# An attention kernel's opening: a load call moved, one root by GpSimd, six roots in two batches

## Chip, cores and metric

The kernel runs on one core of a Trainium2 chip. The metric is the device time of one execution in microseconds (us); lower is better. The engines are TensorE (PE; its weight loads are shown as PEld), VectorE (DVE), ScalarE (ACT) and GpSimd (POOL); SyncE (SP) issues most of the DMA transfers.

## The reference, cut

The input `x` has the shape (2, 256, 128, 128): batch, times, bands, channels, all float32.

```python
xt = _ln(x, ln_t_w, ln_t_b).transpose(0, 2, 1, 3)
x = x + _mha(xt, t_wi, t_bi, t_wo, t_bo, 4, causal_mask).transpose(0, 2, 1, 3)   # over times
xf = _ln(x, ln_f_w, ln_f_b)
x = x + _mha(xf, f_wi, f_bi, f_wo, f_bo, 4, band_mask)                           # over bands
xn = _ln(x, ln_n_w, ln_n_b)
h = gelu(xn @ w1.T + b1)                                                         # 128 -> 512
x = x + (h @ w2.T + b2)
```

`_ln` subtracts the mean over the 128 channels and multiplies by the reciprocal root of the variance plus 1e-5. That reciprocal root is "the root" in what follows.

## The kernel before, in words

The work is cut into groups of 512 tokens (128 partitions, four tiles of 128 channels). There are 128 groups of attention over times (`OverTime`), then, in runs, 128 of attention over bands and 128 of the feed-forward part. This document concerns the first dozen groups. Groups are counted from 0 in the code; "fifth group" is `groups[4]`.

**Loads.** `groups()` walks over the bands with `f0` in steps of `GA = 8`. Eight bands are one *quad*: one tile `x`, shared by four groups. Each of the four calls of `load` fetches 32 of its 128 partitions, so the statistics of any group of a quad need all four transfers. Quad 0 (groups 0 to 3) lies in a constant tile, quad 1 (groups 4 to 7) has `f0 = 8`, quad 2 (groups 8 to 11) has `f0 = 16`. `start` calls the loads of quads 0 and 1, then `load_w1T`, then those of quad 2. All these transfers are issued by SP, which works through its list in order.

**Normalising.** For each group, `statistics` (VectorE: four `bn_stats`, four `bn_aggr`) writes mean and variance to `mv`. The root is made in one of two ways. `root` uses GpSimd (add, then power -0.5) and gives `rstd` at once. `root_by_scalar` uses ScalarE (Ln, then Exp with scale -0.5), and `refine` adds a Newton step of three VectorE instructions. The result of ScalarE can be put into a PSUM bank: `root_in_spare` uses the last columns of the bank called `b2`, `root_in_bank` its first columns. A `Four` joins the statistics of several groups in one tile `mvs`, so that one root and one `refine` serve them all; before the change it is used from group 12 on, for four groups each. The early groups are turned (transposed) by TensorE and copied to `xnT` by VectorE; from group 4 on (`TURNED`) a group goes through VectorE's 32x32 transpose and DRAM (`turned`), and is fetched back as `xnT`.

**Steps.** After `start`, `run` emits one step per `n`. A step interleaves the second half of group n's scores with the first half of group n+1's (`time_scores`), the exponentials (`first_weights`, `second_weights`), masks and adds by GpSimd, the products of the weights with the values of group n-1 (`weigh`), its division (`invert` on ScalarE, `divide` on VectorE), and the query, key and value products of group n+2. Eight PSUM banks are passed round by name; after each step `hand_banks_on` gives the names to other banks, so that the next step's scores go into banks that earlier results have left. All engines' instructions are pinned: each engine works through its list in the order in which the program emits it. Line 900 of the profile is the helper that emits them, so tiles and not lines tell the groups apart.

In step 0 the places concerned are, in this order: the late `second_weights`, the fifth root in spare columns, the TensorE turn of group 2 and its copy, the three small products `fold_output` and `fold_hidden` (weights `t_woT`, `f_woT`, `w1T`), the VectorE results `b` and `orow` of these, and `refine` of the fifth group. `stay_warm(4, ...)` in `start` emits 16 matmuls of one column each, whose result is not read.

Of the kernel before, what the change touches and what calls it, by code (L numbers as in the profile page):

```python
# [10 lines left out]
F32 = mybir.dt.float32  # L11
# [8 lines left out]
P = 128  # L20
# [5 lines left out]
NT = 4  # L26
# [6 lines left out]
BANK = 512  # L33
# [336 lines left out]
class Group:  # L370
# [28 lines left out]
    def means(self):  # L399
        if self.four is None:  # L400
            return self.path.small.tile([P, NT, 2], F32, name="mv", bufs=16)
        if self is self.four.groups[0]:
            self.four.mv = self.path.small.tile([P, NT * NT, 2], F32, name="mvs", bufs=3)
        return self.four.part(self.four.mv, self)

    def root(self):
# [21 lines left out]
    def refine(self):  # L428

        path, vector, y, n = self.path, self.path.vector, self.root0, self.mv.shape[1]  # L430
        t = path.small.tile([P, n], F32, name=f"vy{n}")
        vector.scalar_tensor_tensor(t, self.mv[:, :, 1], EPS, y, ALU.add, ALU.mult)
        vector.scalar_tensor_tensor(t, t, -0.5, y, ALU.mult, ALU.mult)
        self.rstd = path.small.tile([P, n], F32, name="rstd" if n == NT else "rstds", bufs=16 if n == NT else 3)
        vector.scalar_tensor_tensor(self.rstd, t, 1.5, y, ALU.add, ALU.mult)

    def normalize(self):
# [200 lines left out]
def rows_of(h):  # L638
    return slice(h * D, (h + 1) * D)


def product(path, out, weights, x, start=True, stop=True, turn=0):


    for c in range(P // D):
        path.tensor.matmul(out[rows_of(c)], weights[:, rows_of((c + turn) % NT)], x, start=start, stop=stop)
# [258 lines left out]
class BoundedPath:  # L905
# [71 lines left out]
    def groups(self, x, out):  # L977
        nc, k = self.nc, self.k
        B, T, FB, C = x.shape
        NC_T = T // P  # L980
        for b in range(B):
            for f0 in range(0, FB, GA):
                held = {}


                def load(g, f0=f0, b=b, held=held):
                    if b == f0 == 0:
                        held["x"] = k.x0
                        return
                    if g == 0:  # L990
                        self.input_quad(held)
                    f = f0 + g // NC_T * NT
                    self.sync.dma_start(held["x"][rows_of(g)], self.of_times(x[b], g, slice(f, f + NT)))

                def store(g, f0=f0, b=b, held=held):
                    for i in range(NT if g % 2 else 0):
                        f = f0 + i // NC_T * NT + g
                        self.sync.dma_start(
                            self.of_times(k.x1[b], i, slice(f - 1, f + 1)), held["res"][rows_of(i), :, g - 1 : g + 1]
                        )  # L1000

                def part(name, g, i=None, a=0, held=held):
                    if name == "res" and name not in held:
                        self.quad(held, "res", 2)
                    if i is not None:
                        return self.longer(held[name], i * NT + g, a)
                    return held[name][:, :, g]

                for g in range(NT):
                    yield OverTime(self, partial(part, "x", g), partial(part, "res", g), partial(load, g), partial(store, g))  # L1010
        for b in range(B):
            for r0 in range(0, T, RUN):
                run = []
                for t0 in range(r0, r0 + RUN, GB):
                    held = {}


                    def load(g, t0=t0, b=b, held=held):
                        if g == 0:
                            self.input_quad(held)  # L1020
                            self.quad(held, "x2", 2 * RUN // GB)
                        self.sync.dma_start(
                            held["x"][rows_of(g)].rearrange("q g t c -> q (g t) c"),
                            self.of_bands(k.x1[b], t0 + NT * g, NT),
                        )

                    def store(g, t0=t0, b=b, held=held):
                        last = b == B - 1 and t0 == T - GB
                        n = 1 if last and g > 1 else 2
                        for i in range(NT if (g + 1) % n == 0 else 0):  # L1030
                            queue = self.scalar if last and g == NT - 1 and i % 2 else self.sync
                            queue.dma_start(
                                self.of_bands(out[b], t0 + NT * i + g + 1 - n, n),
                                held["res"][rows_of(i), g + 1 - n : g + 1].rearrange("q g t c -> q (g t) c"),
                            )

                    def part(name, g, i=None, a=0, held=held):
                        if name == "res" and name not in held:
                            self.quad(held, "res", 2)
                        if i is not None:  # L1040
                            return self.longer(held[name], g * NT + i, a)
                        return held[name][:, g]

                    run += [(g, part, load, store) for g in range(NT)]
                for g, part, load, _ in run:
                    yield OverBands(self, partial(part, "x", g), partial(part, "x2", g), partial(load, g))
                for g, part, _, store in run:
                    yield FeedForward(self, partial(part, "x2", g), partial(part, "res", g), None, partial(store, g))

    def warm(self, banks):  # L1050


        for i in banks:
# [2 lines left out]
            self.tensor.matmul(  # L1056
                bank, self.k.ones, self.k.ident.unsqueeze(1).to_broadcast([P, n, P]), start=True, stop=True
            )

    def stay_warm(self, n, column):  # L1060
        for i in range(n):
            product(self, column, self.k.ident, self.k.ones[:, 0:1])

    def fold(self, a, engine):

# [129 lines left out]
    def start(self, groups):  # L1195

        first, second, third, fourth, fifth = groups[:5]
        b = self.banks
        for group in groups[: 2 * NT]:
            group.load()  # L1200
        self.k.load_w1T()
        for group in groups[2 * NT : 3 * NT]:
            group.load()
        self.warm((0, 1, 5, 2))
        first.statistics()
        self.fold(0, self.vector)
# [26 lines left out]
        time_scores(None, first)  # L1233
        second.turn_by_tensor(b["b0"], self.vector)
        self.fold_products(1, self.ps[7])
        self.stay_warm(4, self.ps[7][:, BANK - 1 :])
        self.fold_bias(1)
        Attention.place = dict(qp=b["b3"], kp=b["b1"], vp0=b["b0"], vp1=b["b2"])
        first.first_weights(first.early)
# [10 lines left out]
        second.values()  # L1250
        second.take_values()
        fifth.statistics()
        self.hand_banks_on()

    def hand_banks_on(self):
# [5 lines left out]
    def run(self, x, out):  # L1261
        groups = list(self.groups(x, out))

        def do(n, *names):
            if 0 <= n < len(groups):
                for name in names:
                    getattr(groups[n], name)()

        def at(n, kind):
            return 0 <= n < len(groups) and isinstance(groups[n], kind)  # L1270
# [10 lines left out]
        run0 = [i for i in range(len(groups)) if at(i, OverBands)][: RUN // NT]  # L1281
        times = range(3 * NT, run0[-1] + 1)
        fours = {i + NT - 1: Four(self, groups[i : i + NT]) for i in times[::NT]}
        A, k = RUN // NT, self.k
        early = [i for i in range(3, len(groups)) if at(i, FeedForward) and at(i - 3, OverBands)]

# [11 lines left out]
        for n in range(len(groups) + 2):  # L1298
# [8 lines left out]
            do(n, "first_half", "first_function", "first_mask")  # L1307
            if n == 0:
                do(3, "normalize_flat")
            if 0 < n < 3 * NT - 5:  # L1310
                do(n + 5, "statistics")
            if n + 2 * NT in times:
                do(n + 2 * NT, "statistics")
            if old is not None or new is not None:
                time_scores(old, new)
                b = self.banks
# [2 lines left out]
                Attention.place = {}  # L1319
            if old is not None:  # L1320
                old.second_weights(old.late)
                if n == 0:
                    do(4, "root_in_spare")
                if n + 2 < TURNED:
                    groups[n + 2].turn_by_tensor(b["b0"], self.vector)
                if n == 0:
                    self.fold_output(self.ps[b["b3"]])
                    self.fold_hidden(b["b3"])
                    self.add_rows()
                    do(4, "refine")  # L1330
                if n == run0[0] - 1:
                    self.square_queries()
                do(n - 2, "output")
# [7 lines left out]
            if new is not None:  # L1341
                new.first_weights(new.early[1:])
            if n == 1:
                do(5, "root_in_spare", "refine")
            if 0 < n < 3 * NT - 5:
                do(n + 5, "root_in_bank")
            if n + 2 * NT in fours:
                fours[n + 2 * NT].root_in_bank()
            if n == run0[0] - 1:
# [15 lines left out]
            if old is not None:  # L1365
                do(n - 2, "finish")
            if n == 0:
                do(5, "statistics")
            elif n + 5 < 3 * NT:
                do(n + 5, "refine")  # L1370
            if n + 2 * NT in fours:
                fours[n + 2 * NT].refine()
            if not bands[2] and not turn:
# [112 lines left out]
```

## Time and profile before

| | |
|---|---|
| median of 3 runs | 2644.02 us (2640.17 to 2646.56) |
| the profiled execution | 2645.2 us |
| its span, first to last instruction | 2643.3 us |
| granted TensorE clock, mean | 0.998 |
| TensorE busy | 2625.4 us, 99% of the span |
| VectorE / ScalarE / GpSimd busy | 2143.1 / 1839.8 / 1955.0 us |
| DMA | 344.99 MB, mean 131 GB/s |
| loads of `x` by SP (256 KB each) | 124, median 4.4 us to landing |

The page gives totals over the span; the timeline and the windows show stretches of it in us from the first instruction. A bracket such as `[2.07 <-ACT p L900]` tells how long an engine stood idle before the row and which event ended that. "issue" means that the profile shows nothing that the engine waited for.

### The profile page before, as it was taken

To read this page: it belongs to the slowest core of one execution; us is meant where nothing else is said; L and a number is where in the kernel's file an instruction comes from. 1 tells how busy PE (TensorE), PEld (TensorE's weight loads), DVE (VectorE), ACT (ScalarE), POOL (GpSimd) and SP (SyncE) were. 2 spreads that over 40 slices of the span, in tenths; PEclk is the share of its full clock that TensorE was granted. 3 is DMA by queue.
4 is the path that set the end of the run, shared out by engine and by line. 5 is a ranking of instruction groups with operands and counts; after the bars stand their busy time and mean duration, and the time that the engine had idled before them with its cause. 6 is when DMAs were issued, how large, how long until landed. Compare 5 with 4: busy or idle time off the path is not lost.

```text
span 2643.3 us, 156538 instructions
## 1 busy us (share of the span) xinstructions
PE 2625.4 (99%) x68720; PEld 1872.0 (71%) x68720; DVE 2143.1 (81%) x6422; ACT 1839.8 (70%) x3553; POOL 1955.0 (74%) x2309
## 2 busy tenths in 40 slices
PE   8999999999999999999999999999999999999998
PEld 5667667666666666777667777777776777777776
DVE  7888888888888887977878779788797797887974
ACT  6898998988998974664755746647557466475573
POOL 6999999999999986666567666665776666657762
PEclk9999999999999999999999999999999999999999
DMA  5655555656656544444454444444444445444443
GB/s 144 156 148 153 156 145 151 160 147 151 155 149 155 128 126 114 121 126 123 119 125 125 122 121 121 127 124 119 121 122 130 118 115 132 125 116 126 117 107 83
DMA packets 469846, 344.99 MB, mean 131 GB/s; under 512 B 43168, under 2 KB 404512, under 8 KB 469152
## 3 DMA queue, kind: packets, MB, share of 16 engines
q1 hardware_dynamic: 468432, 334.41, 49.9%
q8 instruction: 541, 8.86, 1.5%
q14 instruction: 153, 1.25, 0.2%
q10 hardware_dynamic: 720, 0.46, 0.1%
HBM read 167.98 MB, written 166.72 MB: 127 GB/s over the span
## 4 chain that ended last, share of the span: by engine, by line
PE 99%; DVE 0%; issue 0%; DMA 0%; ACT 0%; ACTq 0%; DVEq 0%
PE bank L900 99%; ACT hT L900 0%; DMA x<-in_x 0%; DMA xnT<-turned 0%; DVE stats L900 0%; DVE res L900 0%; DVE u L900 0%; DVE bank L900 0%; ACT p L900 0%; DVE gs L900 0%; DVE mv L900 0%; DVE z L900 0%; DVE oT L900 0%; DVE xnT L900 0%; DVE vy L900 0%
## 5 line engine op out<-in xcount | busy, mean ns | idle before, releaser
L900 ACT ACTIVATE hT<-bank,b 128x512 f32<-128x512 f32 x512 | 347.7, 688 | 516.2 <-PE bank L900 475.4
L900 POOL TENSOR_SCALAR_AFFINE_SELECT pf<-pf 128x512 f32<-128x512 f32 x768 | 476.6, 634 | 184.5 <-ACT pf L900 158.3
L900 PEld LDWEIGHTS bank<-w2T_sb,hT 128*32 128x32 f32 x16384 | 475.5, 110 | 49.5 <-issue 28.9
L900 PE MATMUL bank<-xnT,wf 128*32 128x512 f32 x4096 | 494.4, 594 | 2.2 <-ACT p L900 2.1
L900 PE MATMUL bank<-xnT,w1f 128*32 128x512 f32 x4096 | 494.5, 592 | 0.0
L900 PE MATMUL bank<-w2T_sb,hT 128*32 128x128 f32 x16384 | 490.3, 273 | 1.2 <-issue 0.6
L900 ACT ACTIVATE p<-bank 128x512 f32<-128x512 f32 (+1 forms) x1024 | 430.8, 494 | 71.7 <-PE bank L900 69.2
L900 DVE TENSOR_SCALAR xh<-x,mv,rstd 128x160 f32<-128x160 f32 (+1 forms) x1040 | 405.3, 432 | 59.8 <-POOL rstd L900 49.3
L900 POOL TENSOR_SCALAR_AFFINE_SELECT p<-p 128x1024 f32<-128x1024 f32 (+2 forms) x384 | 363.4, 946 | 67.8 <-ACT p L900 59.5
L900 PEld LDWEIGHTS bank<-wf,xnT 128*32 128x32 f32 x8192 | 244.1, 110 | 145.0 <-issue 100.6
L900 POOL TENSOR_TENSOR p<-p,p 128x512 f32<-128x512 f32 x256 | 324.1, 1287 | 10.7
L900 DVE BATCH_NORM_STATS2 stats<-x 128x6 f32<-128x128 f32 x1536 | 329.1, 277 | 3.3 <-DMA x<-in_x 3.3
L900 POOL TENSOR_SCALAR rstd<-mv 128x4 f32<-128x4 f32 x250 | 57.1, 228 | 362.9 <-DVE mv L900 361.3
L900 PEld LDWEIGHTS bank<-xnT,w1f 128*32 128x32 f32 x4096 | 206.2, 110 | 153.4 <-issue 94.9
L900 PE MATMUL bank<-qT,kT 32*64 32x80 f32 (+4 forms) x16384 | 305.8, 272 | 2.8 <-issue 2.4
L900 PEld LDWEIGHTS bank<-qT,kT 32*64 32x64 f32 x16384 | 261.9, 131 | 55.4 <-ACT kT L900 50.4
L900 DVE TENSOR_TENSOR res<-bank,res 128x512 f32<-128x512 f32 (+1 forms) x259 | 170.4, 658 | 154.1 <-PE bank L900 149.5
L900 ACT ACTIVATE pf<-bank 128x512 f32<-128x512 f32 x512 | 266.2, 601 | 36.2 <-PE bank L900 31.3
L900 PE MATMUL bank<-wn,oT 128*32 128x128 f32 x8192 | 286.9, 274 | 1.0 <-issue 0.9
L900 DVE STREAM_TRANSPOSE z<-xh 128x512 f32<-128x512 f32 x380 | 270.4, 712 | 13.7
L900 PE MATMUL bank<-wf,xnT 128*32 128x128 f32 x8192 | 277.3, 273 | 0.2 <-DVE rstd L900 0.2
L900 POOL TENSOR_TENSOR rstd<-rstd,mhalf 128x4 f32<-128x4 f32 x250 | 259.5, 1038 | 20.8
(102 smaller groups left out, 3825.5 us busy)
## 6 DMA issues: line engine op xcount, KB each, us to landing
turned<-z SPq DMA_DIRECT2D x1520, 64.0 KB, 2.7
xnT<-turned SPq DMA_DIRECT2D x380, 256.0 KB, 3.1
x<-res SPq DMA_DIRECT2D x256, 128.0 KB, 2.4
x<-x SPq DMA_DIRECT2D x128, 256.0 KB, 4.0
out<-res SPq DMA_DIRECT2D x252, 128.0 KB, 2.4
x<-in_x SPq DMA_DIRECT2D x124, 256.0 KB, 4.4
x<-in_x SPq DMA_DIRECT2D x4, 128.0 KB, 2.8
x<-in_x SPq DMA_DIRECT2D x6, 64.0 KB, 2.5
```

What stands on the lines that cost most here:

```text
L900: return self.tc.keep_in_program_order(emit(*args, **kwargs))
```

## The change

- `stay_warm` and its call are removed.
- The loads of quad 2 are no longer called in `start`, but in step 0, after the TensorE turn of group 2. In `load`, a VectorE memset of one column of the fresh `x` tile is emitted when `f0 == 2 * NT`, that is when `f0 == 8`.
- The fifth group's root is made by GpSimd in `start`; its ScalarE root and its `refine` in step 0 are removed.
- Groups 5 to 7 and groups 8 to 10 form two batches of three, with one root and one `refine` each (steps 1 and 3); group 11 has its own (step 5). The statistics of groups 5 to 11 are emitted at other places: group 5 in step 0 after the turn, 6 and 7 at the end of step 0, 8 in step 1, 9 to 11 in steps 2 to 4.
- The tiles `mvs` and `rstds` are always taken at full size and cut to the number of groups.

```diff
-            self.four.mv = self.path.small.tile([P, NT * NT, 2], F32, name="mvs", bufs=3)
+            mvs = self.path.small.tile([P, NT * NT, 2], F32, name="mvs", bufs=3)
+            self.four.mv = mvs[:, 0 : NT * len(self.four.groups)]
...
                     if g == 0:
                         self.input_quad(held)
+                        if b == 0 and f0 == 2 * NT:
+                            self.vector.memset(held["x"][:, 0, 0, 0:1], 0.0)
...
         self.k.load_w1T()
-        for group in groups[2 * NT : 3 * NT]:
-            group.load()
...
         self.fold_products(1, self.ps[7])
-        self.stay_warm(4, self.ps[7][:, BANK - 1 :])
...
         fifth.statistics()
+        fifth.root()
...
+        threes = [Four(self, groups[i : i + 3]) for i in (5, 8)]
...
-            if 0 < n < 3 * NT - 5:
-                do(n + 5, "statistics")
+            if 1 < n < 5:
+                do(n + 7, "statistics")
...
-                if n == 0:
-                    do(4, "root_in_spare")
                 if n + 2 < TURNED:
                     groups[n + 2].turn_by_tensor(b["b0"], self.vector)
                 if n == 0:
+                    for group in groups[2 * NT : 3 * NT]:
+                        group.load()
+                    do(5, "statistics")
                     self.fold_output(self.ps[b["b3"]])
                     self.fold_hidden(b["b3"])
                     self.add_rows()
-                    do(4, "refine")
...
             if n == 1:
-                do(5, "root_in_spare", "refine")
-            if 0 < n < 3 * NT - 5:
-                do(n + 5, "root_in_bank")
+                threes[0].root_in_spare()
+                threes[0].refine()
+            if n == 3:
+                threes[1].root_in_bank()
+            if n == 5:
+                do(11, "root_in_bank")
...
             if n == 0:
-                do(5, "statistics")
-            elif n + 5 < 3 * NT:
-                do(n + 5, "refine")
+                do(6, "statistics")
+                do(7, "statistics")
+            if n == 1:
+                do(8, "statistics")
+            if n == 3:
+                threes[1].refine()
+            if n == 5:
+                do(11, "refine")
```

More of the change, by code (lines that the diff above doesn't have):

```diff
@@ L433, in refine @@
         vector.scalar_tensor_tensor(t, t, -0.5, y, ALU.mult, ALU.mult)
-        self.rstd = path.small.tile([P, n], F32, name="rstd" if n == NT else "rstds", bufs=16 if n == NT else 3)
+        if n == NT:
+            self.rstd = path.small.tile([P, NT], F32, name="rstd", bufs=16)
+        else:
+            self.rstd = path.small.tile([P, NT * NT], F32, name="rstds", bufs=3)[:, 0:n]
         vector.scalar_tensor_tensor(self.rstd, t, 1.5, y, ALU.add, ALU.mult)
@@ L1058, in warm @@
             )
-    def stay_warm(self, n, column):
-        for i in range(n):
-            product(self, column, self.k.ident, self.k.ones[:, 0:1])
     def fold(self, a, engine):
```

## The prediction

> **What bounds the kernel now.** I read the page first: the span, the busy shares and the chain that ended last. The first line is the profiled execution, the second TensorE's share, the third the chain.
>
> ```profile
> span 2643.3 us, 156538 instructions
> ...
> PE 2625.4 (99%) x68720; PEld 1872.0 (71%) x68720; DVE 2143.1 (81%) x6422; ACT 1839.8 (70%) x3553; POOL 1955.0 (74%) x2309
> ...
> PE 99%; DVE 0%; issue 0%; DMA 0%; ACT 0%; ACTq 0%; DVEq 0%
> ```
>
> TensorE is the bound, so only a stretch where it stands still, or runs slowly, can pay. The change touches steps 0 to 6, so I took TensorE's timeline there next (start, length, operation, idle before).
>
> ```profile
> 14.38 0.43 PE L900 MATMUL bank<-ones,ident 128*32 128x1 f32 x32
> 14.96 1.92 PE L900 MATMUL bank<-xnT,wf 128*32 128x512 f32 x16
> ...
> 17.69 0.93 PE L900 MATMUL bank<-qT,kT 32*64 32x64 f32 x27
> 21.01 1.97 PE L900 MATMUL bank<-qT,kT 32*64 32x256 f32 x37 [2.39 <-issue]
> 22.90 1.83 PE L900 MATMUL bank<-ident,xh 128*128 128x128 f32 x8
> ...
> 25.01 0.95 PE L900 MATMUL bank<-cols_sb,w1T_sb 128*128 128x1 f32 x8
> 28.04 3.45 PE L900 MATMUL bank<-xnT,wf 128*32 128x512 f32 x16 [2.07 <-ACT p L900]
> ...
> 39.42 0.65 PE L900 MATMUL bank<-wf,xnT 128*32 128x128 f32 x16 [0.21 <-DVE rstd L900]
> 40.00 0.66 PE L900 MATMUL bank<-qT,kT 32*64 32x64 f32 x14
> 40.86 1.78 PE L900 MATMUL bank<-qT,kT 32*64 32x256 f32 x50 [0.20 <-DVE u L900]
> ```
>
> There are two large holes, 2.39 us and 2.07 us, and two small ones. From 42.57 us to past 50 us there is none. The windows view (PE, PEld, DVE, ACT, POOL busy; granted clock; DMA share) shows a slow clock after each large hole:
>
> ```profile
> 21.00:24.40 3.40, 3.39 (x44) 2.92 (x44) 0.00 (x0) 1.34 (x5) 0.00 (x0) 0.51 0.75 160
> 24.40:27.80 3.40, 1.56 (x15) 1.48 (x14) 2.31 (x8) 0.88 (x3) 0.23 (x1) 0.99 0.02 5
> 27.80:31.20 3.40, 3.16 (x16) 0.79 (x20) 3.33 (x17) 1.85 (x4) 3.25 (x4) 0.51 0.19 38
> ```
>
> Last, ScalarE's timeline at the second hole:
>
> ```profile
> 23.31 0.29 ACT L900 ACTIVATE lnv<-mv,eps 128x4 f32<-128x4 f32 x1
> 23.63 0.18 ACT L900 ACTIVATE bank<-lnv 128x4 f32<-128x4 f32 x1
> 23.74 0.85 ACT L900 ACTIVATE p<-bank 128x512 f32<-128x512 f32 x2
> 27.11 1.85 ACT L900 ACTIVATE p<-bank 128x256 f32<-128x256 f32 x4 [2.52 <-DVE rstd L900]
> ```
>
> The fifth group's root sits in spare columns of bank b2. The exponential of b2's scores waits until VectorE has refined that root (27.09 us); the refinement queues behind `b`, which waits for the w1T product (25.98 us). TensorE's next query product needs a bank that a later exponential frees.
>
> **What the Trainium skill says.** "Runtime: NRT & Kernel Launch", section "Instruction fetch mechanics": instructions are refilled in 16 KiB blocks of 256 by DMA. The trace agrees: queue q8 moved 541 packets, 8.86 MB, so 16.4 KB each. Counting weight loads and matmuls, the first hole begins after record 448; three later pauses put down to "issue" come after 68288, 91072 and 121536, each a multiple of 256 further. The one q8 packet of the 18 to 19 us window goes out with the DMA engines about full (share over 1 from 10 to 22 us). So the first hole is an instruction fetch behind the input loads. "TensorE: Matmul & The Clock Gate", "What's actually happening": the clock halves after an idle window of about 3.4 us and returns after a busy one. Agrees in length (0.51 over 3.4 us, twice), except that the window before the second slow stretch was 1.56 us busy of 3.40: partial idleness sufficed. Same page, "Architectural detail": ScalarE and VectorE are strict FIFO; the 27.11 line shows it.
>
> **The change part by part.** *Third quad's loads.* I set the two built orders side by side. `f0` steps by 8, so `f0 == 2 * NT` is the **second** quad. The memset lands beside the constants at the top of VectorE's order, and only the second quad's first load gains a wait on it. The nearest rows, memsets of 62 and 59 ns, end by 1.1 us; that load issues at 8.6 us. The third quad's loads keep their place in SP's order, right after w1T, and gain no wait. SP's whole order is unchanged, as are `turned`, `xnT`, stores and all that queue behind them. Cost 0, gain 0, and the fetch stays late: ready at 21.0 us again.
>
> *stay_warm removed.* 32 records (16 matmuls), 0.43 us at 14.38. The product after it waits anyway for VectorE's xnT copy, done at 14.92: gain 0 there. It leaves 0.5 us idle in a 3.4 us window, too little for the clock; lower bound 0, upper bound one slow window (+1.7). I take 0. But record 448 now falls 32 matmul records later in the program. Those (of 37 that ran in 1.89 us at half clock) run before the hole: 1.89 x 32/37 = 1.6 us at half clock, 0.8 at full. After 21.01 the work until the w1T product ended was 3.4 x 0.51 + 1.6 = 3.3 us at full clock; 2.5 is left. The clock is still halved (about 2.0 us idle of 3.4, more idle than the window that halved it the second time), so 1.7 is done by 24.4 and the end comes at **25.2** instead of 25.98.
>
> *Fifth root by GpSimd.* POOL: 0.23 + 1.04 us after its mask (done 19.4), so 20.7; covered by its 8.19 us wait for `p` until 27.57. VectorE needs it at about 25.8. The refinement (3 x 0.16) and ScalarE's 0.29 + 0.18 leave the chain, and b2's exponential no longer waits: the bank of the query product is free at about 22.8 (two 128x256 exponentials, one 128x512, after scores ending near 21.4). The xnT copy follows the turn (ends 23.2) and is done at 24.0. So the product starts at 25.2 instead of 28.04: **-2.84 us**. Bounds: -2.1 (only the hole) and -4.8 (if the first slow window goes too). With TensorE busy from 24.4 to 27.8 the slow stretch after it should go: 3.16 us at half clock, **-1.55 us**, bounds 0 and -1.6.
>
> *Sixth group's statistics ahead of `b`.* Statistics take 1.04 us from start to next start (41.43 to 42.48); between 24.0 and 25.05, before `b`'s product ends at 25.2. Cost 0. The sixth and seventh after the turn fill VectorE until about 30.1; the next turn ends at 34.7 - 4.4 = 30.3: 0.
>
> *First batch of three.* ScalarE does one root instead of two there; ln of 128x16 is 338 ns against 327 of 128x4, so 12 columns cost about the same. It lies in spare columns, so the 0.21 us wait on `rstd` goes. But VectorE's queue before divide(0) loses refine (38.86 to 39.29, 0.43) and gains the ninth group's statistics (1.04): 0.61 later. Behind divide stands `u`, and TensorE waits for `u`: its 0.20 wait becomes 0.20 + 0.21 + 0.61 = 1.0. Net **+0.61**, bounds 0 and +1.3 (if x comes late too).
>
> *Steps 2 to 6.* Four roots fewer on ScalarE (0.5 us each) and VectorE; other statistics one step later, from loaded data. TensorE has no hole there: 0, bounds -0.3 and +0.5.
>
> Sum: -2.84 - 1.55 + 0.61 = **-3.8 us**. The profiled execution took 2645.2 us (span 2643.3 and 1.9 around it), so 2641.4. The median shown, 2644.02, is 1.2 lower: **2640.2**, -0.14%.
>
> **The rivals.** *Fetch pause gone or short.* If the block lands before about 19 us (the third quad being held after all, or its queue draining sooner), 2.0 us of hole and 1.7 of slow clock go too: -7.5, 2636.5. For: DMA is the only obstacle. Against: SP's order is the same. *The hole only changes owner.* VectorE or ScalarE holds the query product until about 27, or the slow clock recurs at 27.8: -1 to -2, about 2642.5. For: a partly idle window halved the clock. Against: the worked times leave 1 to 2 us of slack. *A second fetch exposed (slower).* Record 704 now falls near the end of step 1's scores, at about 29.1 us. The second fetch went out between 24 and 25.5, and the first took effect about 1.6 us after its packet ended (19.4 to 21.0). If it goes out after about 28.5, TensorE stops over 2.4 us and loses 1.6 of clock: all gained is gone; by 2 us later still, 2646. For: TensorE moves forward and DMA does not. Against: the loads end near 22.5.
>
> **How the numbers follow.** 0.2% is 5.3 us, about what a measurement of this kernel can tell from no change. Main case 0.57, of which 0.08 gains over 5.3 us; pause gone 0.26; owner changed 0.10; second fetch 0.07, of which 0.03 with the fetch after it late as well, past 5.3 us slower. Faster 0.08 + 0.26 = 0.34, slower 0.03, same 0.63. Range 2635.8 (all of the first rival, with 0.7 of spread) to 2643.8 (owner changed, worst).
>
> **What would show it.** Right: TensorE's hole to 21.0 still there but 5 score records after it; query product near 25 without a wait on `p`; clock full from 24.4; about 1.0 us wait for `u` near 36 to 37. Wrong: third quad's loads issued after 22 us; the first hole gone; a new "issue" hole near 29; half clock after 27.

## The result, and the profile after

| | before | after |
|---|---|---|
| median, same chip | 2645.99 us (2640.17 to 2653.18) | 2640.77 us (2637.24 to 2647.48) |
| ratio after / before | | 0.9981 (95%: 0.9974 to 0.9988), -5.0 us (-6.9 to -3.2) |
| profiled execution / its span | 2645.2 / 2643.3 us | 2640.7 / 2638.7 us |

The changed kernel is faster by 0.19%. In its page, the span, the engines' busy times and the chain that ended last say the same as before: TensorE is the bound.

```profile
span 2638.7 us, 156452 instructions
...
PE 2622.6 (99%) x68688; PEld 1862.4 (71%) x68688; DVE 2141.0 (81%) x6408; ACT 1838.1 (70%) x3543; POOL 1955.8 (74%) x2311
...
PE 98%; DVE 1%; POOL 0%; issue 0%; ACT 0%; DMA 0%; ACTq 0%; DVEq 0%; POOLq 0%
```

TensorE's timeline after (start, length, operation, idle before and its releaser; the helper's line is now 904):

```profile
15.48 1.92 PE L904 MATMUL bank<-xnT,wf 128*32 128x512 f32 x16 [0.51 <-DVE xnT L904]
...
18.20 1.36 PE L904 MATMUL bank<-qT,kT 32*64 32x64 f32 x59
21.52 0.33 PE L904 MATMUL bank<-qT,kT 32*64 32x128 f32 x5 [1.96 <-issue]
...
24.11 1.93 PE L904 MATMUL bank<-xnT,wf 128*32 128x512 f32 x16
...
36.01 2.52 PE L904 MATMUL bank<-qT,kT 32*64 32x256 f32 x50 [1.22 <-DVE u L904]
38.47 1.93 PE L904 MATMUL bank<-wn,oT 128*32 128x128 f32 x32
```

The first hole is still there, still put down to "issue", and 5 score records follow it where 37 did. The third group's query product starts at 24.11 us with no wait on `p`. The wait for `u` has grown from 0.20 to 1.22 us. The windows view (PE, PEld, DVE, ACT, POOL busy; granted clock; DMA share; GB/s) adds the clock:

```profile
21.00:24.40 3.40, 2.88 (x29) 2.66 (x32) 1.35 (x5) 2.13 (x5) 1.78 (x3) 1.00 0.80 179
24.40:27.80 3.40, 3.40 (x98) 2.14 (x97) 3.33 (x15) 2.19 (x5) 3.32 (x4) 1.00 0.02 7
...
34.60:38.00 3.40, 2.18 (x52) 1.81 (x50) 3.26 (x13) 0.42 (x2) 1.81 (x2) 0.84 0.80 177
38.00:41.40 3.40, 3.40 (x66) 2.33 (x60) 2.58 (x6) 1.96 (x6) 1.25 (x2) 0.66 0.40 132
```

Both slow stretches of before are gone, the one after the first hole too. A new one stands behind the wait for `u`, from about 36.9 to 40.3 us.

**Where the time went.** I lay the two traces over each other at the start of the second group's query product (14.96 before, 15.48 after) and read the distance to three later rows.

| stretch | before | after | difference |
|---|---|---|---|
| to the third group's query product | 13.08 | 8.63 | -4.45 |
| from there to the first output product (`wn,oT`) | 14.53 | 14.36 | -0.17 |
| from there to the sixth output product, five steps | 36.44 | 36.27 | -0.17 |
| sum | 64.05 | 59.26 | **-4.79** |

The last row is two things that nearly cancel. Output products follow each other after 7.08, 7.08, 7.27, 7.50 and 7.51 us before, and after 7.95 and four times 7.08 us after. So the slow clock costs 0.87 us in the first step, and the three later steps gain 1.04 us. That the sum comes close to the measured -5.0 is partly luck: in another execution of the same code, below, the first hole is 0.8 us shorter.

### The profile page after: what moved, and what is told of

It is laid out like the page before. It is cut to its first block, busy times and chain, and to the rows that moved or that the text cites. A ratio compares the mean times of both kernels' runs of the same rounds, so it can differ in the third digit from the quotient of the medians.

```text
span 2638.7 us, 156452 instructions
## 1 busy us (share of the span) xinstructions
PE 2622.6 (99%) x68688; PEld 1862.4 (71%) x68688; DVE 2141.0 (81%) x6408; ACT 1838.1 (70%) x3543; POOL 1955.8 (74%) x2311
## 4 chain that ended last, share of the span: by engine, by line
PE 98%; DVE 1%; POOL 0%; issue 0%; ACT 0%; DMA 0%; ACTq 0%; DVEq 0%; POOLq 0%
PE bank L904 98%; POOL rstd L904 0%; DVE stats L904 0%; DVE xh L904 0%; DMA x<-in_x 0%; DVE ln L904 0%; ACT hT L904 0%; DMA xnT<-turned 0%; ACT p L904 0%; DVE z L904 0%; DVE u L904 0%; POOL res L904 0%; POOL x L904 0%; DVE mv L904 0%; DVE res L904 0%
## 5 line engine op out<-in xcount | busy, mean ns | idle before, releaser
L904 DVE TENSOR_SCALAR xh<-x,mv,rstd 128x160 f32<-128x160 f32 (+1 forms) x1016 | 395.9, 432 | 59.5 <-POOL rstd L904 49.3
L904 PEld LDWEIGHTS bank<-xnT,w1f 128*32 128x32 f32 x4096 | 200.6, 110 | 158.9 <-issue 89.9
```

The lines of the kernel that those rows point to most:

```text
L904: return self.tc.keep_in_program_order(emit(*args, **kwargs))
```

## The experiments

All ratios are to the kernel before, on the same chip. "Local" is the time from the second group's query product to the first output product in the one profiled execution of each kernel (27.61 us before, 22.99 after).

| kernel | ratio (95%) | local, us |
|---|---|---|
| before + fifth root by GpSimd | 0.9996 (0.9989 to 1.0003) | 23.68 |
| before without `stay_warm` | 0.9984 (0.9977 to 0.9990) | 25.19 |
| after, third quad truly held | 0.9966 (0.9954 to 0.9978) | 20.06 |
| after, ninth statistics later | 0.9975 (0.9963 to 0.9986) | 20.94 |
| both of these | 0.9963 (0.9950 to 0.9977) | 18.95 |
| after, again | 0.9982 (0.9972 to 0.9992) | 21.43 |
| before, third quad truly held | 0.9982 (0.9975 to 0.9989) | 22.06 |
| before, `stay_warm` moved | 0.9992 (0.9983 to 1.0000) | 25.58 |
| after, root undone | 0.9992 (0.9985 to 0.9998) | 28.38 |
| after, `stay_warm` put back | 0.9991 (0.9984 to 0.9998) | 22.44 |
| before + root, without `stay_warm` | 0.9979 (0.9972 to 0.9987) | 27.25 |

### One part alone: the root

```diff
         fifth.statistics()
+        fifth.root()
...
-                if n == 0:
-                    do(4, "root_in_spare")
...
-                    do(4, "refine")
```

> The kernel before, with one part of the change: the fifth group's root is made by GpSimd in the start, and its ScalarE root and refinement in step 0 are left out. stay_warm and all else stay. Theory (the root in b2's spare columns made the second hole): the first hole stays at about 2.4 us with some 37 score records behind it; the 2.07 us hole in front of the third group's query product is gone, the product starts near 26.0, and no slow clock follows it; the waits near the first division stay small, 0.2 to 0.3 us each. Gain 2.0 (hole) to 3.6 us (with the slow window). Rival A (stay_warm's removal and the batches carry the gain): the hole keeps at least half of its length because another releaser takes over, gain below 1 us. Rival B (all of the measured 5 us comes from this one part): gain about 5 us.

Measured: median 2648.29 against 2648.76 us, -1.1 us (-2.9 to +0.8). TensorE's timeline:

```profile
20.90 1.12 PE L900 MATMUL bank<-qT,kT 32*64 32x256 f32 x37 [2.12 <-issue]
...
25.81 1.93 PE L900 MATMUL bank<-xnT,wf 128*32 128x512 f32 x16
```

The 2.07 us wait on `p` is gone, as it should be. The local stretch is 3.9 us shorter, yet the timed gain is not told from none: this run alone does not size the root. Half clock still follows the first hole, as before.

### One part alone: stay_warm

```diff
-        self.stay_warm(4, self.ps[7][:, BANK - 1 :])
```

> The kernel before without the 16 one-column matmuls of stay_warm; all else stays. Theory (they only move the instruction at which the first fetch is waited for): the first hole still ends when the block has landed, within 1 us of where it ended before and begins some 0.5 us later; about 5 score records stand behind it instead of 37; the second hole of about 2 us stays. Gain 0.8 us, between 0 and 1.6. Rival A (they keep the clock up): a slow stretch appears before 18 us and the kernel is 1 to 2 us slower. Rival B (16 matmuls of plain TensorE time): gain 0.4 us, with the hole as long as before.

Measured: 2645.42 against 2648.76 us, -4.2 us (-6.1 to -2.6). TensorE's timeline:

```profile
20.86 0.33 PE L900 MATMUL bank<-qT,kT 32*64 32x128 f32 x5 [1.68 <-issue]
...
25.59 3.04 PE L900 MATMUL bank<-xnT,wf 128*32 128x512 f32 x16 [2.08 <-ACT p L900]
```

Record 448 has moved as worked out (5 records after the hole), the hole is 1.68 us and no half clock follows it. The second hole and the slow stretch after it (the product takes 3.04 instead of 1.92 us) stay, since they belong to the root. The gain is larger than the 0 to 1.6 us expected: that sum had left out the slow stretch after the first hole, 1.7 us.

### The third quad held in fact

```diff
-                        if b == 0 and f0 == 2 * NT:
+                        if b == 0 and f0 == 4 * NT:
```

> The changed kernel with the memset's condition at f0 == 4 * NT, so that the third quad's loads, and the two loads behind them in SP's list, really wait for VectorE behind the turned copy of the third group. Theory (the first hole is an instruction fetch behind the third quad's traffic): SP issues those loads after 20 us; the DMA engines fall idle near 16 to 17 us; the first hole shrinks from about 2.0 us to under 0.3 us; gain over the changed kernel 2 us, up to 3.7 if a slow window went with it. Rival A (the hole is no fetch, or the fetch is slow by itself): the hole stays near 2 us. Rival B (the traffic only moves): another hole put down to issue opens between 24 and 36 us, where the third or fourth block is fetched behind the moved loads, or VectorE waits for x in the ninth group's statistics; gain near 0 or a loss of up to 3 us.

Measured: 2640.84 against 2648.76 us, -9.0 us (-12.2 to -5.8), 4 us ahead of the changed kernel, give or take 3.7. The issues on SP's list, first in the kernel before, then in the changed kernel, then here:

```profile
10.98 4.84 SPq L900 DMA_DIRECT2D x<-in_x  x6
```

```profile
11.03 5.37 SPq L904 DMA_DIRECT2D x<-in_x  x6
```

```profile
10.29 0.43 SPq L904 DMA_DIRECT2D w1T_sb<-in_w1T  x1
21.29 3.79 SPq L904 DMA_DIRECT2D x<-in_x  x6
```

With `f0 == 16` the memset lands in VectorE's order behind the second turned copy (it runs at 21.19 us), the load waits for it, and SP has nothing out between w1T and 21.29 us. From 18 to 20 us the DMA engines move nothing, where they are over full in the changed kernel (229 GB/s). The 16 KB block of instructions goes out at 16.41 us, against 18.53 in the changed kernel, and lands before TensorE has run out. TensorE's timeline shows it:

```profile
17.89 1.46 PE L904 MATMUL bank<-qT,kT 32*64 32x64 f32 x64
...
21.61 1.92 PE L904 MATMUL bank<-xnT,wf 128*32 128x512 f32 x16
```

All 64 score records run in one go; the first hole does not exist. So input loads ahead of the block made the hole, and the change as given did not hold the third quad back.

### The ninth group's statistics later

```diff
-            if n == 1:
-                do(8, "statistics")
...
             do(n - 1, "divide")
+            if n == 1:
+                do(8, "statistics")
```

> The changed kernel with the ninth group's statistics emitted behind the first division instead of ahead of it, nothing else. Theory (those 1.04 us stand in front of u on VectorE): the wait of TensorE for u at step 2 falls from 1.22 us to about 0.2 to 0.4 us, and the slow stretch behind it, where the profile shows one, goes: gain over the changed kernel 0.8 us, up to 2.5 with the slow stretch. Rival (the wait comes from the batched refinement or from ScalarE's late reciprocal): the wait stays above 0.8 us and the time is the same within 0.3 us.

Measured: 2642.50 us, -6.6 us (-9.8 to -3.7). VectorE's timeline in the changed kernel shows the row that was in the way, and TensorE's timeline of this kernel that the wait is gone:

```profile
33.44 0.83 DVE L904 BATCH_NORM_STATS2 stats<-x 128x6 f32<-128x128 f32 x4
34.19 0.36 DVE L904 BATCH_NORM_AGGREGATE mvs<-stats 128x2 f32<-128x6 f32 x4
34.47 0.67 DVE L904 TENSOR_TENSOR bank<-bank,r 128x512 f32<-128x512 f32 x1
35.18 0.69 DVE L904 SCALAR_TENSOR_TENSOR u<-bank,r 128x512 f32<-128x512 f32 x1
```

```profile
34.34 1.78 PE L904 MATMUL bank<-qT,kT 32*64 32x256 f32 x50 [0.19 <-DVE u L904]
```

The statistics hold VectorE from 33.44 until 34.47 us, 1.03 us, and `u` is that much late. Behind `divide` they delay nobody: the wait is back to 0.19 us. In time, the gain over the changed kernel (0.9975 against 0.9981) lies inside the intervals.

### Both together

```diff
-                        if b == 0 and f0 == 2 * NT:
+                        if b == 0 and f0 == 4 * NT:
...
-            if n == 1:
-                do(8, "statistics")
...
             do(n - 1, "divide")
+            if n == 1:
+                do(8, "statistics")
```

> The changed kernel with both edits of e3 and e4: the third quad's loads really held behind the third group's turned copy, and the ninth group's statistics behind the first division. Theory (fetch behind the loads, and statistics ahead of u, are separate costs): no hole near 19 to 21 us, wait for u at step 2 at 0.2 to 0.4 us; the product of the first group's output starts near 34.4 us, against 35.2 in e3 and 36.1 in e4. Gain over the changed kernel on this chip about 3.5 us (2.5 to 5). Rival (the statistics now wait for x, loaded late, and the division stands behind the next step): gain no larger than e3's alone.

Measured: 2639.00 against 2647.70 us, -9.8 us (-13.2 to -6.1): the lowest ratio here, though not told from the third quad held alone. One new wait for data appears in TensorE's timeline:

```profile
38.19 1.92 PE L904 MATMUL bank<-xnT,wf 128*32 128x512 f32 x16 [0.49 <-DMA xnT<-turned]
```

The stores of `turned` now queue behind the held loads (between 20 and 40 us a median of 5.4 us to landing, against 3.9 in the changed kernel), so a later group's `xnT` comes 0.49 us late.

The local stretch ends too early to show the whole price. The six steps behind it take 45.7 us here, 44.5 with the third quad held alone and 42.5 in the changed kernel run again. From the second group's query product to the end of these six steps the three profiles differ by less than 1 us (64.7, 64.6 and 63.9 us). So where the timed lead of the held kernels over the changed kernel comes from is not shown.

### The changed kernel again, and the third quad held in the kernel before

The first of the next two is the changed kernel with no edit. The second is the kernel before with the loads moved and truly held, and nothing else:

```diff
                     if g == 0:
                         self.input_quad(held)
+                        if b == 0 and f0 == 4 * NT:
+                            self.vector.memset(held["x"][:, 0, 0, 0:1], 0.0)
...
-        for group in groups[2 * NT : 3 * NT]:
-            group.load()
...
                 if n == 0:
+                    for group in groups[2 * NT : 3 * NT]:
+                        group.load()
                     self.fold_output(self.ps[b["b3"]])
```

> The changed kernel as it is, beside the experiments on the same chip. Theory: 4 to 6 us below the kernel before, the sum of e1 and e2 (0.5 to 1.5 and 3.3 to 4.2 us) less the longer wait for u; slower than e3 by 2 to 4 us and than e4 by about 1 us. Rival (the parts interact): more than 7 or less than 2.5 us below before.

> The kernel before with one part of what the change is described as: the third quad's load calls moved to step 0 and the memset put on the third quad, so that they are held; stay_warm, the roots and the statistics stay as before. Theory (first hole = fetch behind the third quad's traffic): the hole of 2.4 us at 18.6 us is under 0.3 us and no slow clock follows it; the second hole of 2.07 us on the fifth root stays, with its slow stretch; gain 2.4 to 4.5 us. Rival A (without the first hole the second one grows, because ScalarE and VectorE were hidden by it): the second hole is 3 us or longer and the gain under 2 us. Rival B (held loads delay a later fetch): a hole put down to issue between 22 and 36 us.

Measured: the changed kernel again 2641.51 against 2647.70 us, -4.8 us (-7.4 to -2.1), which repeats the result. In its profile the first hole is 1.14 us instead of 1.96 and no slow stretch follows the wait for `u`. The kernel before with the quad held: 2643.38 us, -4.8 us (-6.6 to -2.9). Its timeline:

```profile
17.64 1.93 PE L900 MATMUL bank<-qT,kT 32*64 32x64 f32 x64
...
23.96 1.92 PE L900 MATMUL bank<-xnT,wf 128*32 128x512 f32 x16 [2.08 <-ACT p L900]
```

The first hole is gone but for a remainder inside the row (1.93 us for the 64 records, 1.46 above). The second stays, without a slow stretch after it. So the intended move of the loads, by itself, gained as much as all that the change did, within the errors.

### Was it the records, or the 16 matmuls?

`stay_warm` could cost by its own 0.43 us or by where it puts record 448. Here it stays in the program but behind the hole:

```diff
-        self.stay_warm(4, self.ps[7][:, BANK - 1 :])
...
                     self.fold_hidden(b["b3"])
+                    self.stay_warm(4, self.ps[b["b3"]][:, BANK - 8 : BANK - 7])
```

> The kernel before with the 16 matmuls of stay_warm moved from the start to the place behind the fold products of step 0, in front of the third group's query product, where TensorE waits for ScalarE anyway. Every instruction from there on has the same position in TensorE's program as in the kernel before. Theory (e2's gain comes from what runs ahead of the first fetch, in the first 30 us): same picture as e2 with 59 score records ahead of the hole and no slow window behind it, gain 2.5 to 4.5 us as e2's. Rival (e2's gain comes from the later block boundaries, which moved by 64 instructions over the whole kernel): gain under 1.5 us.

Measured: 2646.15 against 2647.70 us, -2.1 us (-4.5 to 0.0), between what the two expected: undecided in time. The trace has the picture of the kernel without `stay_warm`: 5 records after a hole of 1.41 us and full clock behind it. The moved matmuls take 0.43 us in their new place with 0.33 us of waiting ahead, and VectorE's `orow` waits 0.62 us for them, with the fifth group's `refine` behind it. That is a cost which `stay_warm` does not have in its old place, so this run does not settle the question.

### Each part undone in the changed kernel

The root back on ScalarE, and, separately, the 16 matmuls back in their place:

```diff
-        fifth.root()
...
+                if n == 0:
+                    do(4, "root_in_spare")
...
+                    do(4, "refine")
```

> The changed kernel with the fifth group's root taken back to ScalarE and b2's spare columns, with its refinement behind the row sums as before; the rest of the change stays. Theory (that root made the second hole): a hole of about 2 us, ended by an exponential, is back in front of the third group's query product near 25 us, sometimes with a slow stretch; the wait for u at step 2 keeps about 1.2 us; 2 to 3.5 us slower than the changed kernel, so 1.5 to 3 below the kernel before. Rival (e1's small gain in the timed runs is all that this part is worth): within 1 us of the changed kernel, 4 us or more below the kernel before.

```diff
         self.fold_products(1, self.ps[7])
+        for i in range(4):
+            product(self, self.ps[7][:, BANK - 1 :], self.k.ident, self.k.ones[:, 0:1])
```

> The changed kernel with the 16 matmuls of stay_warm put back in the start. Theory (they decide how much work stands behind the first fetch): about 37 score records stand behind the first hole again, the hole is about 0.5 us longer and a slow stretch follows it; 0.8 to 2.5 us slower than the changed kernel, so 2.5 to 4 below the kernel before. Rival (e2's gain of 4 us is theirs alone): 4 us slower than the changed kernel, within 1 us of the kernel before.

Measured: 2641.50 and 2639.83 against 2642.72 us, -2.1 us (-4.0 to -0.5) and -2.4 us (-4.2 to -0.5). Against the changed kernel's -5.0, undoing the root gives back about 2.9 us and putting `stay_warm` back about 2.6, each by some 2.5 us either way. TensorE's timeline with the root undone has the second hole again:

```profile
27.93 3.29 PE L904 MATMUL bank<-xnT,wf 128*32 128x512 f32 x16 [2.07 <-ACT p L904]
```

The half clock behind it is not of its own making in this profile: it began at 20.51 us, with a first hole of 2.41 us, and ran on to 30.75. With `stay_warm` put back, 37 records stand behind the first hole again, but no slow stretch follows, against the expectation:

```profile
20.18 1.07 PE L904 MATMUL bank<-qT,kT 32*64 32x256 f32 x37 [1.84 <-issue]
```

So what `stay_warm` costs is measured in time by two runs, and this profile does not show it. Within these errors the parts add up: root alone and `stay_warm` alone sum to -5.3 us, too.

### The batches of three

The traces differed in steps 4 to 6, where the prediction had put nothing. So the two parts above were made together, without the batches:

```diff
-        self.stay_warm(4, self.ps[7][:, BANK - 1 :])
...
         fifth.statistics()
+        fifth.root()
...
-                if n == 0:
-                    do(4, "root_in_spare")
...
-                    do(4, "refine")
```

> The kernel before with two parts of the change: fifth root by GpSimd in start, and stay_warm removed; the load calls and the roots and statistics of groups 5 to 11 stay as before. Theory: without the batches of three the fourth to sixth later steps keep VectorE full, since the statistics of a single group and of a batch of four fall into the same step, so TensorE's period from one output product (wn,oT) to the next is again 7.27, 7.50 and 7.50 us instead of 7.08 (+1.04 us in all against the changed kernel); in exchange the wait for u near 34 us is back to about 0.2 us (-1.0). So the time is that of the changed kernel within the error: ratio to before 0.998, 0.9973 to 0.9988. Rival: the longer periods belong to something that the batches do not touch (a late transfer, the fifth root), and they are 7.08 here: then the ratio is about 0.9977 and the periods tell it.

Measured: 2644.68 against 2650.17 us, -5.6 us (-7.4 to -3.4), the changed kernel's gain within the error. Output products follow after 7.08, 7.08, 7.61, 7.50 and 7.51 us, and TensorE waits 0.21 us for `u`. (The local stretch of 27.25 us holds a first hole of 2.98 us and some ten us of half clock in this one execution.) Both halves of the theory hold: the batches shorten three later steps, and pay for it by the wait for `u`. The three long steps, of 7.27 to 7.61 us, stand in this profile and in the five before it that lack the batches. In the changed kernel, in its repetition and with either part undone, the same steps take 7.08 us.

What paces those steps was tried in the kernel before, by leaving out two thirds of the refinement of groups 9 to 11:

```diff
+    def take_root(self):
+        path, vector, y, n = self.path, self.path.vector, self.root0, self.mv.shape[1]
+        self.rstd = path.small.tile([P, n], F32, name="rstd", bufs=16)
+        vector.scalar_tensor_tensor(self.rstd, self.mv[:, :, 1], 0.0, y, ALU.mult, ALU.add)
...
             elif n + 5 < 3 * NT:
-                do(n + 5, "refine")
+                do(n + 5, "refine" if n < 4 else "take_root")
```

> The kernel before, but the Newton step of three VectorE instructions for groups 9 to 11 (steps 4 to 6) is replaced by one VectorE instruction that only copies ScalarE's root: the refinement of these three groups is left out. ScalarE's work is unchanged. Theory (VectorE paces these steps): two instructions of 0.14 to 0.16 us less, with 0.17 us from start to start, so the three periods of 7.27, 7.50 and 7.50 us become 7.08, about 7.2 and about 7.2. Rival (ScalarE paces them, with its root of 0.5 us in each): they stay at 7.27, 7.50 and 7.50. The time of one run tells nothing at this size.

One profiled execution, of 2653.4 us. The windows view of one such step, first before, then here (columns as above):

```profile
64.00:71.50 7.50, 7.50 (x193) 5.09 (x192) 7.22 (x29) 6.47 (x16) 6.72 (x7) 1.00 0.54 142
```

```profile
70.36:77.44 7.08, 7.08 (x199) 4.91 (x192) 6.87 (x27) 6.52 (x16) 6.56 (x7) 1.00 0.62 152
```

All five steps take 7.08 us. ScalarE's work did not change (6.47 and 6.52 us); VectorE lost two instructions, 7.22 to 6.87 us. So VectorE paced these steps. The late opening of this execution (first output product at 49.12 us) is no rival: the kernel without batches opened nearly as late, at 46.27, and kept its long steps. TensorE's waits were spread inside the score rows (1.81 us for 64 records instead of 1.39), each too small to be listed as a wait. From start to start the three instructions had held VectorE's list for 0.44 us, and the single one holds it for 0.07. VectorE's own period, from one `u` to the next, falls from 7.50 to 7.12 us, so 0.38 of the 0.42 us are accounted for, more than the 0.3 expected.

## Why the prediction was right, and where it was off

It gave 2640.2 us and -0.14%; measured were 2640.77 us and -0.19%, beside a before of 2645.99. The predicted gain of 3.8 us lies inside the measured interval. That the two times agree within 0.6 us is luck: the prediction started from a median of three runs, 2 us below the later one. By its steps:

- **Third quad's loads: cost 0, gain 0, fetch stays late.** Right. SP's rows are those of before, and the hole ends at 21.52 us. Holding the quad in fact removes the hole. The rival of the pause gone put that at 7.5 us below before; the held version measured -9.0 us (-12.2 to -5.8).
- **stay_warm: the records move across the hole.** Right in the mechanism: 5 records instead of 37. The term that failed is the slow window after the first hole, which was left in place ("the clock is still halved"). With a hole of 1.96 us instead of 2.39 it did not come (the last section shows how busy TensorE was there), so the w1T product started at 23.23 us and the query product at 24.11, not 25.2. Over the same stretch -4.45 us were read where -2.84 were worked out; the 1.6 between them is one slow window (3.4 us at half clock). This was the bound of -4.8 that the prediction named and did not take.
- **Fifth root by GpSimd.** Right: its power took 1.04 us, ended at 21.06, and nobody waited for it. The wait on `p` went, and the slow stretch after it.
- **First batch of three, +0.61.** The wait for `u` was 1.22 us against the 1.0 worked out. What was not foreseen is that such a wait can halve the clock again: in this profile it did, for 0.74 us lost before the first output product (the 50 score records took 2.52 us, 1.78 elsewhere) and 0.87 after. In four other profiles with a wait of 1.16 to 1.23 us (the changed kernel again, the third quad held, and each part undone) it did not.
- **Steps 2 to 6: 0.** Wrong, by -1.04 us, outside the bounds of -0.3 and +0.5. I looked for holes in TensorE's timeline and found none; the loss lay inside rows, and showed only in the distance from one step to the next. With the wait for `u` it nearly cancels, so the batches are worth about nothing.
- **Second fetch exposed.** Did not come. In the profile after, the first pause of TensorE put down to "issue" after that of record 448 follows record 14272. (These counts take in TensorE's sequencer, which the prediction does not say: in the trace before, 443 weight loads and matmuls and six of the sequencer's instructions start ahead of the first hole.)

The two misses of 1.6 and 1.0 us in favour and the one slow stretch of 1.6 us against left the sum close to the prediction. It was the right answer with two terms mis-sized. What stays open is why the root alone gained only 1.1 us, what `stay_warm` cost beyond the place of record 448, and the few places where the clock did not follow TensorE's busy share (last section).

## What to carry to other kernels

A load call that was moved in the program moved no transfer here, because nothing made the transfer wait: look at the issuing queue's own rows, and at which tile a guard really hits. Pauses with no releaser that lie multiples of 256 records apart point to instruction fetches; here a gap on the DMA engines ahead of one removed it. Measure steps by the distance between like rows, not only by listed waits: a pacer that is a few per cent too slow leaves no hole.

## What the runs showed of the hardware that was not expected

- **Idle time and half clock.** In the profiles, first holes of 2.12 us and more were followed by half clock (2.12, 2.39, 2.41, 2.98 and 3.42 us), those of 1.96 us and less were not (1.96, 1.84, 1.69, 1.68, 1.41, 1.14 us). The second hole, 1.97 to 2.08 us, began at full clock in four profiles: half clock followed in three, and not with the third quad held in the kernel before. The wait for `u`, of 1.2 us, was followed by it in one of five. The Trainium skill ("TensorE: Matmul & The Clock Gate", "What's actually happening") gives an idle window of about 3.4 us as the cause, and a busy one as what ends it. Here some 2 us of idleness sufficed; the measurement decides.
- **What separates the cases better than the length of a hole.** Within each of the fourteen traces, all changes of the clock lie whole multiples of 3.41 us apart. These points cut a trace into stretches of 3.41 us, and what separates the cases is how busy TensorE was in each. Of the 17 stretches at full clock in which it was busy for less than half, 14 were followed by half clock; of the other 10,751, one was. Two stretches of the kernel before, both followed by half clock, then two of the changed kernel (columns as above):

```profile
17.51:20.92 3.41, 1.11 (x39) 0.55 (x28) 2.71 (x11) 1.06 (x4) 1.87 (x3) 1.00 1.08 222
24.34:27.75 3.41, 1.62 (x15) 1.54 (x14) 2.26 (x8) 0.89 (x3) 0.18 (x1) 1.00 0.02 5
```

```profile
19.84:23.25 3.41, 1.73 (x18) 1.66 (x18) 0.94 (x4) 1.98 (x6) 1.77 (x3) 1.00 1.03 225
33.49:36.90 3.41, 2.19 (x64) 1.57 (x61) 3.27 (x14) 1.52 (x4) 2.92 (x3) 1.00 1.04 244
```

The third, 1.73 us busy, kept the clock: 0.28 us of the hole of 1.96 us fell into the stretch before it. The fourth, 2.19 us busy, is the one exception, and it stays open. Slow stretches lasted one, two, three or four times 3.41 us. Of ten stretches at half clock with TensorE busy throughout, seven were followed by full clock; after the 2.98 us hole, that from 28.96 to 32.37 us was not.

- **Pauses of TensorE put down to "issue".** They recur through the whole kernel. In the fourteen profiles there are 111 of them, and every one lies a multiple of 256 records from record 448. They add up to 1.9 to 6.6 us in a profile and change from one execution to the next (3.5 and 2.9 us in two of the changed kernel). The Trainium skill ("Runtime: NRT & Kernel Launch", "Instruction fetch mechanics") calls the cost of such a boundary mostly hidden. That holds for nearly all of them here, but not behind queued input loads.
- **One profile does not rank such kernels.** The fastest profiled execution of all was that of the changed kernel with `stay_warm` put back, 2637.0 us; its median ratio is 0.9991. Outside the local stretch the profiled executions, on different chips, took from 2612.5 us (`stay_warm` put back) to 2622.9 us (without batches), a spread wider than any gain here.
